# A three-tap convolution by four products for two outputs, in a transformer block on one core

## The chip, the core and the metric

One Trainium2 chip, one core. TensorE (PE, with its weight loads PEld), VectorE (DVE), ScalarE (ACT), GpSimd (POOL) and SyncE's DMA queue (SP) each work through their own list in order and wait for one another by semaphores. The time is that of one launch in device microseconds (us), median of three runs. All data are float32.

## The reference

Eight sequences of 512 tokens, width 256, 16 heads of 16. The block is: layer norm, causal attention, a convolution over the context whose output is a second query, a second attention with the same keys and values, an output projection; then a feed-forward part with a third attention and a mixture of eight experts, two per token. What the change touches is this:

```python
ctx = _causal_attn(q, k, v)
ctx_c = ctx.reshape(b, s, d).transpose(0, 2, 1)
conv_out = jax.lax.conv_general_dilated(ctx_c, conv_w, window_strides=(1,), padding=[(1, 1)],
                                        dimension_numbers=('NCH', 'OIH', 'NCH')) + conv_b[None, :, None]
q2 = conv_out.transpose(0, 2, 1).reshape(b, s, NUM_HEADS, HEAD_DIM)
ctx2 = _causal_attn(q2, k, v)
```

With x the context as a row of columns, padded by a zero column on each side, and g0, g1, g2 the three 256 x 256 taps, output n is g0 x[n] + g1 x[n+1] + g2 x[n+2].

## The kernel before, in words

Sequences are worked in four pairs, 0 to 3; in a pair, `one` has lane 0 and `two` lane 1. `next0` is the first sequence of the next pair, `before1` the second of the pair before. A pair takes 27 turns, and all attention and everything around it lies in these 108 turns. The experts' products follow behind the last turn.

A turn holds two attention steps. Each sequence has three attentions of nine steps, and the two of a pair alternate: `one`'s first attention is turns 0 to 4 and a half, `two`'s first until turn 9, `one`'s second until turn 13 and a half, `two`'s second until turn 18, then the third ones. A step is scores on PE (`sc`, L1201), in two halves, each into one of two score banks; Exp on ACT (L1208), two of 128x1024; a mask on the diagonal blocks on POOL (L1216). The product with the values (`av`, L1134) of earlier steps comes one turn later, between the turn's two score groups. So PE's order in a turn is: scores, AV, `first_units`, scores, `units`. The order on PE, ACT, DVE and POOL is exactly the order in which the program writes the instructions; nothing is moved by a scheduler.

All other work is cut into units, which `plan(turn, sequence, what, ...)` puts into a turn. `among=first_units` puts a unit ahead of the turn's second scores, otherwise it comes behind them. `follow` puts off a piece of work by some turns to one of three places: "mid" (behind AV), "late" (ahead of the units), "end" (behind them).

- When an attention's chunk (of two, 128 rows of the context each) has all its AV, `normalise` copies the two sums out by ACT (L1151), and three DMAs on SP swap halves of their rows (L1159, L1160). `finish` on DVE then does two reciprocals (L1164) and two products (L1165) on 128x256 each: for chunk 0 in the next turn at "mid", for chunk 1 in the same turn at "end". `check` on ACT (L1168) reads the reciprocals; for chunk 1 it stands at "mid" of the next turn, ahead of that turn's second pair of Exps.
- `conv` is six products per output chunk (two input chunks, three taps, L1366) of a 128x128 weight and 512 columns, all into one bank, and one eviction on DVE with the bias (L1374). The six are spread over turns, so the bank is held (`hold_bank`), and the other units have a single bank while it is. Chunk 0 of q2 is needed at the second attention's first step, chunk 1 at its fifth.
- Units of the next sequence: `stats`, `normed` (DVE, L1311), `transpose` (PE L1281, copied by ACT L1285), `q` (PE L1046, DVE L1343), `k` (PE L1046, two on ACT L1330), `values` (PE L1064, DVE L1082). Units of the sequence before: `transpose3`, `route` (PE L1035, then some twenty small DVE operations and one Exp on ACT, L1535), `slots` (PE L1564 and L1565, sixteen small DVE operations, L1567 to L1579). `slots` leaves eight indirect DMAs (L1588) that POOL issues one after each later mask.
- `h` adds the third attention's projection to the rows; the squares for the norm behind it are ACT's (L1502).

An fp32 product is two records of PE in the profile, with a weight load each; half as many matmuls are written as the counts show.

Of the kernel before, what the change touches and what calls it, by code (L numbers as in the profile page):

```python
# [11 lines left out]
F32 = mybir.dt.float32  # L12
# [611 lines left out]
def fast_path(  # L624
# [221 lines left out]
    with ExitStack() as att:  # L846
# [37 lines left out]
        load_x(1)  # L884
        conv_sb = wp.tile([P, DC, 3, D], F32, tag="conv", name="conv_sb")
        context_rows(conv_sb.rearrange("p c k o -> p c (k o)"), convT.rearrange("d k o -> d (k o)"))
        convb_sb = column(conv_b, D, "convb_sb")
# [95 lines left out]

        free_banks = [0, 1]

        def mm_tile():

            i = free_banks.pop(0)
            free_banks.append(i)
            return ps_mm.tile([P, 512], F32, tag=f"mm{i}", name="mm")  # L990

        def hold_bank():
            i = free_banks.pop(0)
            return i, ps_mm.tile([P, 512], F32, tag=f"mm{i}", name="mm")

# [20 lines left out]
        def table(n):  # L1016
            ps = mm_tile()
            for i in range(NC // 2):
                nc.tensor.transpose(ps[:, i * P : (i + 1) * P], rope[0][:, n * NC // 2 + i], ident)
            half = slice(n % 2 * S // 2, (n % 2 + 1) * S // 2)  # L1020
            nc.scalar.copy((cosT, sinT)[n // 2][:, half], ps[:, : S // 2])


# [83 lines left out]
        def follow(turns, f, where):  # L1107
            due[where].append([turns, f])
# [8 lines left out]

        def attention(qT, kT, v, to):

# [24 lines left out]
            def normalise(ch):  # L1144
# [25 lines left out]
                for n0 in range(0, S, S // 2):  # L1170
                    follow(1 - ch, lambda n0=n0: finish(n0), ("mid", "end")[ch])
                follow(3 - 2 * ch, check, ("late", "mid")[ch])

# [70 lines left out]
        class Batch:  # L1244
# [33 lines left out]
            def transposed(self, d, to, of, scale=None, soon=False):  # L1278
                ps = mm_tile()
                for c in range(NC):  # L1280
                    nc.tensor.transpose(  # L1281
                        ps[:, c * P : (c + 1) * P], of[:, c, d * P : (d + 1) * P], ident
                    )
                if scale is None:
                    nc.scalar.copy(to[:, d, :S], ps)  # L1285
                elif soon:
                    nc.vector.tensor_scalar(  # L1287
                        to[:, d, :S], ps, scale[:, d : d + 1], None, ALU.mult
                    )
                else:  # L1290
                    nc.scalar.mul(to[:, d, :S], ps, scale[:, d : d + 1])
# [28 lines left out]

            def transpose(self, d):
                self.transposed(d, self.xT, self.xn)

# [24 lines left out]
            def attention1(self):  # L1348
# [3 lines left out]
                nc.gpsimd.memset(cx[:, :, S + 1 : S + 2], 0.0)  # L1352
                return attention(self.qT, self.kT, self.v, cx[:, :, 1 : S + 1])

            def conv(self, ch, first, n):

                if ch == 0 and first == 0:
                    self.q2T = self.q_tile("q2T")
                    self.held = {}
                if first == 0:  # L1360
                    self.held[ch] = hold_bank()
                bank, ps = self.held[ch]
                terms = [(d, k) for d in range(DC) for k in range(3)]
                for t in range(first, first + n):
                    d, k = terms[t]
                    nc.tensor.matmul(  # L1366
                        ps,
                        conv_sb[:, d, k, ch * P : (ch + 1) * P],
                        self.cx[:, d, k : k + S],
                        start=(t == 0),  # L1370
                        stop=(t == len(terms) - 1),
                    )
                if first + n == len(terms):
                    nc.vector.tensor_scalar(  # L1374
                        self.q2T[:, ch, :], ps, convb_sb[:, ch : ch + 1], None, ALU.add
                    )
                    free_banks.append(bank)

# [113 lines left out]
            def h(self, half):  # L1492
# [7 lines left out]
                for c in range(2 * half, 2 * half + 2):  # L1500
                    squares = small.tile([P, D], F32, tag="squares", name="squares", bufs=1)
                    nc.scalar.activation(  # L1502
                        squares, self.rows[:, c, :D], AF.Square, accum_out=self.ss[:, c : c + 1]
                    )
# [121 lines left out]
        for p in range(B // 2 + 1):  # L1626
# [14 lines left out]
            plan(t + 4, before1, "transpose3", 0, 1)  # L1641
            plan(t + 5, one, "conv", (0, 0, 2), among=first_units)
            plan(t + 5, one, "conv", (0, 2, 1))
            if next0 is not None:
                plan(t + 6, next0, "transpose", 0)
                plan(t + 6, one, "conv", (0, 3, 3))
                plan(t + 6, next0, "transpose", 1)
                plan(t + 6, before1, "route")
                plan(t + 7, one, "conv", (1, 0, 4))
                plan(t + 8, one, "conv", (1, 4, 2))  # L1650
                plan(t + 8, next0, "k", 0)
                plan(t + 9, next0, "q", 0)
                plan(t + 9, next0, "k", 1)
            else:
                plan(t + 6, one, "conv", (1, 0, 3))
                plan(t + 7, one, "conv", (0, 3, 3))
                plan(t + 7, before1, "route")
                plan(t + 8, one, "conv", (1, 3, 3))
            plan(t + 8, before1, "slots")
            plan(t + 10, next0, "values", 0, 1)  # L1660
            for c in range(NC):
                plan(t + 10 + c, one, "bias", c)
                plan(t + 14 + c, two, "bias", c)
            if next0 is not None:
                plan(t + 11, two, "conv", (0, 0, 4))
                plan(t + 12, two, "conv", (0, 4, 2), among=first_units)
                plan(t + 12, two, "conv", (1, 0, 2))
                plan(t + 13, two, "conv", (1, 2, 2))
                plan(t + 14, two, "conv", (1, 4, 1), among=first_units)
                plan(t + 14, two, "conv", (1, 5, 1))  # L1670
            else:
                plan(t + 9, two, "conv", (0, 0, 2))
                plan(t + 10, two, "conv", (0, 2, 1), (1, 0, 1))
                plan(t + 11, two, "conv", (1, 1, 2))
                plan(t + 12, two, "conv", (0, 3, 2), among=first_units)
                plan(t + 12, two, "conv", (0, 5, 1))
                plan(t + 13, two, "conv", (1, 3, 1))
                plan(t + 14, two, "conv", (1, 4, 1), among=first_units)
                plan(t + 14, two, "conv", (1, 5, 1))
            plan(t + 15, one, "x1", 0, 1)  # L1680
# [40 lines left out]
        plan(0, one, "k", 1)  # L1721
        plan(0, one, "q", 1)
        for v in va[1:]:
            units[1].append(lambda v=v: nc.vector.memset(v, 1.0))
# [228 lines left out]
```

## Time and profile before

| what | us |
|---|---|
| three runs | 1468.43, 1470.07, 1470.27 (median 1470.07) |
| the profiled execution | 1469.26, of which the span of instructions is 1467.5 |
| from the first scores to the first product of the experts | 19.7 to 888.6 |
| turns 5 to 14 of pair 0 | 60.29 to 137.90 |
| of pair 1 | 276.73 to 357.57 |
| of pair 2 | 496.71 to 576.61 |
| of pair 3 | 715.47 to 788.68 |

The granted clock is 0.989 over the run. In the stretch of pair 1 (277 to 358), PE is busy for 80.6 of 81 us, ACT 52.3, POOL 36.6 and DVE 34.7. How to read it: a share of busy time says which engine has the most work in all. What a change is worth is read from the starts of the instructions in the turns that it touches. [...]

### The profile page before, as it was taken

The page shows a single profiled execution, that of the slowest core. Times are in us where ns is not written, and L with a number is a line of the kernel's source. Part 1 is how long each engine was busy: PE and PEld are TensorE (multiplying, and loading weights), DVE is VectorE, ACT ScalarE, POOL GpSimd, SP SyncE. Part 2 cuts the span into 40 slices and gives each one's busy share as a digit, 9 for nine tenths or more (in the row PEclk, how much of TensorE's full clock was granted, in tenths as well). Part 3 has the DMA queues.
Part 4 walks back from the last instruction along what each step waited for, and adds up shares of the span by engine and source line. Part 5 has one row for each costly group of instructions (what it writes and reads, how often), then busy time and mean ns, then how long its engine had stood idle before and what let it go on. Part 6 is the DMA issues. An engine that isn't in the chain of part 4 may idle for free. (4 is left out here: it accounts for less than half of the span.)

```text
span 1467.5 us, 31773 instructions
## 1 busy us (share of the span) xinstructions
PE 1420.6 (97%) x13370; PEld 895.6 (61%) x13370; DVE 675.5 (46%) x1318; ACT 726.5 (50%) x1172; POOL 576.9 (39%) x620
## 2 busy tenths in 40 slices
PE   7999999999999999999999999999999999999995
PEld 4555556555556555556555556667767677676673
DVE  4533886553886553886444865322222212222221
ACT  4666677766777766778766784211211211112110
POOL 2333343635333635333645335443332332333322
PEclk9999999999999999999999999999999999999998
DMA  5112122201001211011212022333131313132200
GB/s 145 57 68 79 67 79 85 82 34 42 23 24 52 96 38 38 23 63 38 86 42 76 13 84 68 112 100 96 54 112 44 111 58 98 61 102 88 87 20 17
DMA packets 62840, 97.61 MB, mean 67 GB/s; under 512 B 13516, under 2 KB 39064, under 8 KB 62688
## 3 DMA queue, kind: packets, MB, share of 16 engines
q1 hardware_dynamic: 52608, 69.74, 14.4%
q0 software_dynamic: 10080, 25.74, 5.3%
q8 instruction: 107, 1.75, 0.5%
q14 instruction: 45, 0.37, 0.1%
HBM read 46.06 MB, written 32.61 MB: 54 GB/s over the span
## 5 line engine op out<-in xcount | busy, mean ns | idle before, releaser
L1208 ACT ACTIVATE pr<-sc 128x1024 f32<-128x1024 f32 x432 | 419.1, 1025 | 155.9 <-PE sc L1201 155.6
L1216 POOL TENSOR_TENSOR pr<-pr,seen 128x512 f32<-128x512 f32 (+1 forms) x216 | 253.9, 1176 | 468.2 <-ACT pr L1208 467.8
L762 PE MATMUL pgu<-xgT,gu 128*128 128x384 f32 x1056 | 348.2, 489 | 0.4 <-DVE hT L777 0.3
L762 PEld LDWEIGHTS pgu<-xgT,gu 128*128 128x128 f32 x1056 | 201.2, 191 | 136.3 <-issue 1.5
L776 ACT ACTIVATE sg<-pgu 128x384 f32<-128x384 f32 x120 | 58.9, 491 | 415.6 <-PE pgu L762 415.6
L1134 PE MATMUL av<-pr,va 64*32 64x512 f32 (+7 forms) x6144 | 217.3, 408 | 0.2 <-POOL pr L1216 0.2
L1201 PE MATMUL sc<-qT,kT 32*128 32x448 f32 (+7 forms) x2048 | 194.7, 439 | 6.5 <-ACT pr L1208 5.4
L1164 DVE RECIPROCAL r<-r 128x256 f32<-128x256 f32 x96 | 167.5, 1745 | 57.7 <-DMA r<-cs 57.6
L786 PE MATMUL po<-dn,hT 128*128 128x256 f32 x864 | 190.9, 379 | 1.9 <-POOL hT L757 1.9
L803 POOL DMA_INDIRECT out_dram<-so_far,xg x72 | 72.5, 1006 | 288.5 <-DVE so_far L793 226.1
L777 DVE TENSOR_TENSOR hT<-sg,pgu 128x384 f32<-128x384 f32 x120 | 66.4, 553 | 250.9 <-ACT sg L776 250.9
L786 PEld LDWEIGHTS po<-dn,hT 128*128 128x128 f32 x864 | 162.4, 190 | 23.9 <-POOL hT L757 2.3
L1134 PEld LDWEIGHTS av<-pr,va 64*32 64x32 f32 x6144 | 113.5, 106 | 101.4 <-issue 71.8
L1201 PEld LDWEIGHTS sc<-qT,kT 32*128 32x128 f32 x2048 | 118.3, 185 | 84.9 <-issue 32.8
L793 DVE SCALAR_TENSOR_TENSOR so_far<-po,xg,so_far 128x256 f32<-128x256 f32 x72 | 34.8, 483 | 150.4 <-PE po L786 150.4
L1201 PE MATMUL sc<-q2T,kT 32*128 32x448 f32 (+7 forms) x1024 | 97.3, 434 | 0.7
L748 POOL DMA_INDIRECT so_far<-out_dram,xg x72 | 74.0, 1028 | 53.5 <-issue 51.7
L1366 PE MATMUL mm<-cx,conv_sb 128*128 128x512 f32 x192 | 94.4, 615 | 0.0
L1201 PEld LDWEIGHTS sc<-q2T,kT 32*128 32x128 f32 x1024 | 60.4, 184 | 45.8 <-ACT pr L1208 19.0
L1588 POOL DMA_INDIRECT xtab<-rows,slot x64 | 65.2, 1019 | 36.5 <-DVE pick L1577 19.5
L1046 PE MATMUL mm<-xT,wqkv_sb 128*128 128x512 f32 x128 | 63.7, 629 | 0.0
L1046 PE MATMUL mm<-xaT,wqkv_sb 128*128 128x512 f32 x128 | 61.3, 612 | 2.0 <-DVE xaT L1287 2.0
(159 smaller groups left out, 1284.6 us busy)
## 6 DMA issues: line engine op xcount, KB each, us to landing
r<-cs SPq DMA_DIRECT2D x96, 128.0 KB, 2.0
xtab<-pad SPq DMA_DIRECT2D x24, 397.5 KB, 3.5
xg<-xtab SPq DMA_DIRECT2D x24, 397.5 KB, 3.1
gu<-in_wg_dram SPq DMA_DIRECT2D x18, 352.0 KB, 3.2
cs<-cs SPq DMA_DIRECT2D x48, 128.0 KB, 2.0
gu<-in_wu_dram SPq DMA_DIRECT2D x18, 320.0 KB, 4.1
dn<-in_wd_dram SPq DMA_DIRECT2D x9, 640.0 KB, 4.7
out_dram<-x SPq DMA_DIRECT2D x9, 512.0 KB, 3.0
```

What stands on the lines that cost most here:

```text
L748: nc.gpsimd.indirect_dma_start(out=so_far[:, s, :], out_offset=None, in_=out, in_offset=token_of(xg, s), bounds_check=B * S - 1, oob_is_er ...
L762: nc.tensor.matmul(ps, gu[d][:, n0 : n0 + P], xgT[:, d, :], start=(d == 0), stop=(d == DC - 1),)
L777: nc.vector.tensor_mul(hT[k], sg, pu)
L786: nc.tensor.matmul(po, hT[k][:, s * P : (s + 1) * P], dn[:, k, :], start=(k == 0), stop=(k == NK - 1),)
L803: nc.gpsimd.indirect_dma_start(out=out, out_offset=token_of(xg, s), in_=so_far[:, s, :], in_offset=None, bounds_check=B * S - 1, oob_is_er ...
L1046: nc.tensor.matmul(ps, w[:, d, n0 : n0 + P], srcT[:, d, :S], start=(d == 0), stop=(d == DC - 1),)
L1134: nc.tensor.matmul(av[i][g * HP : (g + 1) * HP, j * KB :], v[rows, j, ch * G + g, :], pr[rows, g, at : at + n], start=(j == 0), stop=(j == ...
L1164: nc.vector.reciprocal(r[:, half], r[:, half])
L1201: nc.tensor.matmul(sc[:, g - g0, at : at + S - j * KB], kT[r0 : r0 + HP, ch, j], qT[r0 : r0 + HP, ch, j * KB : S], start=True, stop=True,)
L1208: nc.scalar.activation(pr[:, g0 : g0 + 2], sc, AF.Exp, scale=SCALE)
L1216: nc.gpsimd.tensor_tensor(diag, diag, seen.unsqueeze(1).unsqueeze(1).to_broadcast([P, G, len(parts), KB]), ALU.mult,).ins
L1366: nc.tensor.matmul(ps, conv_sb[:, d, k, ch * P : (ch + 1) * P], self.cx[:, d, k : k + S], start=(t == 0), stop=(t == len(terms) - 1),)
```

## The change

Two outputs, an even and an odd one, are made of four products of half the columns. With a, b, c, d four neighbouring columns of the context, the terms are a - c, b + c, d - b, c - b, and the weights g0, (g0 + g1 + g2)/2, g2, (g0 - g1 + g2)/2. The output of the even column is M0 + M1 + M3, that of the odd column M1 - M3 + M2. DVE makes the terms (`differences`, four operations on 128x256 with inputs at a step of two) when a chunk of the first attention is finished. The weights are made once, in turn 2 of pair 0. In `conv`, ACT copies M1 out with the bias, DVE makes M1 + M3 and M1 - M3, then adds M0 and M2 into the columns of q2.

A conv's products (four per bank) are no longer spread, no bank is held, and the two banks of units alternate always. The transposes of the next sequence are copied by DVE instead of ACT in turn 5. The terms of `one` take the buffer of the next sequence's keys, those of `two` the buffers of `rows` and `xn` of lane 0. The squares of `h` go into the bank of the projection instead of a buffer of their own.

```diff
-        conv_sb = wp.tile([P, DC, 3, D], F32, tag="conv", name="conv_sb")
+        conv_sb = wp.tile([P, DC, 4, D], F32, tag="conv", name="conv_sb")
...
-        free_banks = [0, 1]
+        banks = itertools.count()
 
         def mm_tile():
-            i = free_banks.pop(0)
-            free_banks.append(i)
-            return ps_mm.tile([P, 512], F32, tag=f"mm{i}", name="mm")
-
-        def hold_bank():
-            i = free_banks.pop(0)
-            return i, ps_mm.tile([P, 512], F32, tag=f"mm{i}", name="mm")
+            return ps_mm.tile([P, 512], F32, tag=f"mm{next(banks) % 2}", name="mm")
...
+        def conv_weights():
+            g = [conv_sb[:, :, k] for k in range(4)]
+            nc.vector.tensor_tensor(g[3], g[0], g[2], ALU.add)
+            nc.vector.tensor_tensor(g[3], g[3], g[1], ALU.subtract)
+            nc.vector.scalar_tensor_tensor(g[1], g[1], 2.0, g[3], ALU.mult, ALU.add)
+            for k in (1, 3):
+                nc.vector.tensor_scalar(g[k], g[k], 0.5, None, ALU.mult)
...
                 for n0 in range(0, S, S // 2):
                     follow(1 - ch, lambda n0=n0: finish(n0), ("mid", "end")[ch])
+                if then is not None:
+                    follow(1 - ch, lambda: then(ch), ("mid", "end")[ch])
                 follow(3 - 2 * ch, check, ("late", "mid")[ch])
...
-                    nc.scalar.copy(to[:, d, :S], ps)
+                    (nc.vector.tensor_copy if soon else nc.scalar.copy)(to[:, d, :S], ps)
...
+            def differences(self, d):
+                if self.lane == 0:
+                    tag = f"kT{2 - self.set}"
...
+                else:
+                    tag = ("rows0", "xn0")[d]
+                    t = big.tile([P, 4, S // 2], F32, tag=tag, name="terms", bufs=1)
...
+                nc.vector.tensor_tensor(t[:, 0], even[:, :n], even[:, 1:], ALU.subtract)
+                nc.vector.tensor_tensor(t[:, 1], odd[:, :n], even[:, 1:], ALU.add)
+                nc.vector.tensor_tensor(t[:, 2], odd[:, 1:], odd[:, :n], ALU.subtract)
+                nc.vector.tensor_tensor(t[:, 3], even[:, 1:], odd[:, :n], ALU.subtract)
 
-            def conv(self, ch, first, n):
+            def conv(self, ch, pair):
...
+                ps = mm_tile().rearrange("p (k n) -> p k n", k=2)
+                for i, k in enumerate(((1, 3), (0, 2))[pair]):
+                    for d in range(DC):
+                        nc.tensor.matmul(
+                            ps[:, i],
+                            conv_sb[:, d, k, ch * P : (ch + 1) * P],
+                            self.terms[d][:, k],
+                            start=(d == 0),
+                            stop=(d == DC - 1),
+                        )
+                if pair == 0:
+                    m1 = small.tile([P, S], F32, tag="t0", name="t0", bufs=3)[:, : S // 2]
+                    nc.scalar.activation(
+                        m1, ps[:, 0], AF.Identity, bias=convb_sb[:, ch : ch + 1]
                     )
+                    t = self.m = small.tile([P, 2, S // 2], F32, tag="t1", name="t1", bufs=2)
+                    for i, op in enumerate((ALU.add, ALU.subtract)):
+                        nc.vector.tensor_tensor(t[:, i], m1, ps[:, 1], op)
+                else:
+                    to = self.q2T[:, ch].rearrange("p (n i) -> p i n", i=2)
+                    for i in range(2):
+                        nc.vector.tensor_tensor(to[:, i], self.m[:, i], ps[:, i], ALU.add)
...
-            plan(t + 5, one, "conv", (0, 0, 2), among=first_units)
-            plan(t + 5, one, "conv", (0, 2, 1))
             if next0 is not None:
-                plan(t + 6, next0, "transpose", 0)
-                plan(t + 6, one, "conv", (0, 3, 3))
-                plan(t + 6, next0, "transpose", 1)
+                plan(t + 5, next0, "transpose", (0, True), (1, True), among=first_units)
+                plan(t + 5, next0, "q", 0)
                 plan(t + 6, before1, "route")
-                plan(t + 7, one, "conv", (1, 0, 4))
-                plan(t + 8, one, "conv", (1, 4, 2))
-                plan(t + 8, next0, "k", 0)
-                plan(t + 9, next0, "q", 0)
-                plan(t + 9, next0, "k", 1)
             else:
-                plan(t + 6, one, "conv", (1, 0, 3))
-                plan(t + 7, one, "conv", (0, 3, 3))
-                plan(t + 7, before1, "route")
-                plan(t + 8, one, "conv", (1, 3, 3))
-            plan(t + 8, before1, "slots")
-            plan(t + 10, next0, "values", 0, 1)
+                plan(t + 5, before1, "route", among=first_units)
+            plan(t + 7, one, "conv", (0, 0), (0, 1))
+            plan(t + 8, one, "conv", (1, 0), (1, 1))
+            plan(t + 9, next0, "k", 0)
+            plan(t + 9, before1, "slots")
+            plan(t + 10, next0, "values", 0)
+            plan(t + 11, next0, "values", 1)
...
-            if next0 is not None:
-                plan(t + 11, two, "conv", (0, 0, 4))
...
+            plan(t + 12, two, "conv", (0, 0), among=first_units)
+            plan(t + 12, two, "conv", (0, 1))
+            plan(t + 13, next0, "k", 1)
+            plan(t + 14, two, "conv", (1, 0), among=first_units)
+            plan(t + 14, two, "conv", (1, 1))
```

## The prediction

> **What bounds the kernel now.** I read the page's shares first, then the timeline of PE, then those of ACT and DVE where PE waits.
>
> ```profile
> PE 1420.6 (97%) x13370; PEld 895.6 (61%) x13370; DVE 675.5 (46%) x1318; ACT 726.5 (50%) x1172; POOL 576.9 (39%) x620
> ...
> L1366 PE MATMUL mm<-cx,conv_sb 128*128 128x512 f32 x192 | 94.4, 615 | 0.0
> ```
>
> PE is the bound, and the convolution is 94.4 us of it. But ends of matmuls are modelled, so waits hide in a busy PE. I therefore go by starts in the timeline (columns: start, length, engine, line, tiles, count):
>
> ```profile
> 363.56 3.72 PE L1035 MATMUL mm<-outw_sb,c 128*128 128x256 f32 x16
> 367.21 1.14 PE L1201 MATMUL sc<-q2T,kT 32*128 32x512 f32 x8
> ...
> 770.34 1.98 PE L1366 MATMUL mm<-cx,conv_sb 128*128 128x512 f32 x4
> 772.26 1.17 PE L1201 MATMUL sc<-q2T,kT 32*128 32x384 f32 x16
> 773.36 1.12 PE L1366 MATMUL mm<-cx,conv_sb 128*128 128x512 f32 x2
> 774.59 2.05 PE L1201 MATMUL sc<-q2T,kT 32*128 32x320 f32 x16
> 776.58 3.41 PE L1134 MATMUL av<-pr,va 64*32 64x512 f32 x96
> ```
>
> Sixteen products of 256 columns take 3.65 us from start to next start (363.56 to 367.21), four of 512 take 1.92, two 1.24. Scores (L1201) of one step take 1.10, but 1.99 (774.59 to 776.58) when only 1.24 us of other work stood before them: they need the score bank that the step before filled, and ACT's Exp of it must end. From the first score of a step to the last of the next pass about 4.33 us (1.10 + 1.24 + 1.99), or 1.10 + 1.91 + 1.34. So "filler plus next scores" is never under 3.23 us: PE work taken out below 2.1 us of filler saves nothing.
>
> ```profile
> 756.63 1.94 ACT L1208 ACTIVATE pr<-sc 128x1024 f32<-128x1024 f32 x2 [1.32 <-PE sc L1201]
> 759.79 0.63 ACT L1168 ACTIVATE cs<-r 128x512 f32<-128x512 f32 x1 [1.23 <-issue]
> ...
> 760.42 1.92 ACT L1208 ACTIVATE pr<-sc 128x1024 f32<-128x1024 f32 x2
> ```
>
> ```profile
> 752.45 0.15 DVE L1567 TENSOR_TENSOR at<-run,mm 128x8 f32<-128x8 f32 x1
> ...
> 755.49 0.17 DVE L1579 CAST slot<-red 128x4 int32<-128x4 f32 x1
> 755.57 1.75 DVE L1164 RECIPROCAL r<-r 128x256 f32<-128x256 f32 x1
> 757.56 0.48 DVE L1165 TENSOR_TENSOR cx<-cs,r 128x256 f32<-128x256 f32 x1 [0.24 <-DMA cs<-cs]
> 757.97 1.74 DVE L1164 RECIPROCAL r<-r 128x256 f32<-128x256 f32 x1
> ```
>
> This is turn 10 of the last pair (scores at 755.37). ACT's check L1168 needs both reciprocals and stands in ACT's order ahead of the turn's second pair of Exps: slots on DVE 3.1 us, then 4.2 us from the first reciprocal to the check, then 0.63 to the Exps.
>
> **The change, part by part.** Times of turns 5 to 14 before, from first score to first score of turn 15: pairs 0 to 3 take 77.6 (60.29 to 137.90), 80.8 (276.73 to 357.57), 79.9 (496.71 to 576.61) and 73.2 (715.47 to 788.68).
>
> *Products.* A pair has 48 conv records of 512 columns and gets 64 of 256. In a run, starts are 0.43 apart for 512 columns (weight loads at 74.95, 75.38, 75.81) and 0.216 for 256 ((3.65 - 0.2)/16, 0.2 being what a run adds: 1.92 - 4 x 0.43). That is 20.6 against 13.8 us per pair, 27 us over four pairs: the whole possible gain. New blocks: eight records 1.92, sixteen 3.65.
>
> *The new order, turn by turn, for the middle pairs 1 and 2* (scores, AV, scores, units; rows of the same turn before, 1.34 for scores behind a filler of 1.9):
> - 5: 2.04 + 1.02 + 1.24 (eight transposes) + wait 1.6 + 1.10 + q 1.91 = 8.9 (before 7.3).
> - 6: 1.34 + 2.90 + 1.10 + route 1.88 = 7.2 (before 11.9, with transposes queueing for one bank).
> - 7: 1.34 + 1.46 + 1.83 + 3.65, + 0.3 = 8.6 (8.9 and 8.0).
> - 8: 1.10 + 2.31 + 1.10 + 3.65 = 8.2 (8.5).
> - 9: 1.07 + 1.94 + 1.34 + k and slots 2.3 = 6.6 (8.0).
> - 10 and 11: 1.10 + 1.88 + 1.53 + 1.9, then 1.34 + 1.94 + 1.27 + 1.9 = 12.9, + wait 2.9 = 15.8 (16.1).
> - 12, 13, 14: 6.9, 7.7, 7.3 (6.7, 7.6, 5.8), and turn 15 opens with 1.34 instead of 1.98.
> Sum 77.2 - 0.6 = 76.6: a gain of 4.2 and 3.3.
>
> *The wait in turn 5.* The four differences of a chunk stand on DVE between the reciprocals and normed:
>
> ```profile
> 278.37 0.43 DVE L1165 TENSOR_TENSOR cx<-cs,r 128x256 f32<-128x256 f32 x1
> 278.71 1.38 DVE L1311 TENSOR_SCALAR xn<-x,mv,rstd 128x256 f32<-128x256 f32 x4
> ```
>
> One costs 0.43 as L1165 alone does, at 0.45 spacing 1.8 us. Normed ends at 281.9 instead of 280.1; the transposes, now in turn 5 right behind AV (279.79), need it. Scores can start at 282.65 instead of 281.03: 1.6 us. Queued behind on DVE are the two new xT copies (0.65 each) and q; PE needs the copies only after 1.10 of scores. In pair 0 normed would end at 60.2 (58.4 before) for an AV that ends at 63.4; pair 3 has no next chunk.
>
> *The 0.3 in turn 7.* Reciprocals now queue behind q's eviction and end 5 us into turn 6, so the second chunk's differences end about 1 us into turn 7, route's chain starts there, and ACT's small Exp of route (L1535, waits for DVE) holds the score Exps behind it.
>
> *The wait in turn 10.* Slots move to turn 9's end, directly ahead of the reciprocals. With t the first score of turn 10: slots end t + 3.15, check at t + 7.35, Exps t + 8.0 to 9.9, scores of turn 11 end t + 10.65 where 7.75 was due: 2.9. Pair 3 has less filler (due 9.33), so 1.3. Pair 0 has no slots, and its scores lose nothing. Slots' eight indirect transfers on POOL (L1588, 1.02 each, one behind each mask) move with it from turns 9 to 12 into 10 to 13: with two masks (1.27) and a bias (0.74) POOL then has 5.3 us per turn, and the shortest such turn is 5.75 in pair 3. If that cover were gone, AV would wait for its mask.
>
> *Pair 0:* 7.3, 5.35 (no unit in turn 6), 10.15 (scores 3.23 for it), 8.2, 6.3, 6.65, 6.45, 6.9, 7.7, 7.3 = 72.2, less 0.6: gain 6.0. *Pair 3:* turns 6, 10, 11 and 13 have no unit, so 3.23 each time: 6.0, 7.2, 9.7, 8.2, 4.95, 6.1, 6.5, 8.7, 5.75, 9.2 = 72.3, + 1.3 - 0.6: gain 0.2.
>
> *Costed at nothing, with the cover:* making the weights (five operations of 512 elements, about 2.9 us) lies in DVE's gap 38.8 to 43.3; without it values' eviction in turn 2 is that late. The m1 copy on ACT (0.37 as L1021) and the four half adds per chunk (0.43 to 0.48 by L1165 and L793, against one 0.75) end 2 us or more before their bank or q2T is asked for. Squares into PSUM keep 0.42 each (L1502) and hold the bank until then; turn 3's q comes about 1 us after. The terms share buffers: with the next chunk's k, which on PE comes behind the last product that reads them; with rows, whose transfers are through two turns before; with xn, read in turn 5 and rewritten in 9. No wait from these as long as the turns keep this order; else DVE's differences would be late by a transfer, 2 to 3 us. Bounds for all this together: -1 to +3.
>
> Sum: 4.2 + 3.3 + 6.0 + 0.2 = 13.7; I take back 0.6 for DVE operations that meet a mask on POOL in turn 5 (0.75 instead of 0.43 below). From 1469.3 for the profiled run (span 1467.5 and 1.8 around it) that is 1456; the median of 1470.07 lies 0.8 higher, so 1457.
>
> ```profile
> 69.42 0.75 DVE L1165 TENSOR_TENSOR cx<-cs,r 128x256 f32<-128x256 f32 x1 [0.26 <-DMA cs<-cs]
> ```
>
> *Bounds of a difference.* L1165 spans 0.424 to 1.473 us. No row reads two operands at step 2; L954 reduces 128 elements at step 2 in 0.275, L950 the same number in rows of eight in 0.279, so I take no stride cost, nearest 0.43. At 1.47 turn 5 is 4.2 later and turn 7 about 3.5 in two pairs, and pair 0 some 1.
>
> [...]
>
> **The rivals.**
> - *The waits hide, all arithmetic comes through* (20%). If normed and slots were not the last to arrive, 3.2 + 5.8 + 1.3 + 0.6 + 0.6 come back: 1446. For it: before, the check in turn 10 of pair 1 came without idle. Against: in pair 3 it held the Exps, as shown.
> - *Each pair loses 3 us more at the Exp floor* (10%): 1469, no change. For: ACT's order is strict, and turns get shorter while its work stays. Against: ACT is busy 52 of 81 us there.
> - *POOL holds every difference* (8%), slower: each waits for a mask or an indirect transfer. Price 2 x (4.2 + 3.5) + 1 = 16.4 over the forecast: 1473.5; it decides from about 1.4 us per difference. For: L1165's maximum. Against: its median, 0.427.
> - *Half-long products do not hide their weight load* (4%), slower: loads take 0.19 and 256 columns 0.216. At 0.32 instead of 0.216 per record, 256 records cost 27 us more: 1484. For: only 26 ns of slack. Against: L1035 and L786 run at 0.216.
>
> **How the numbers follow.** The forecast, 1457, has 56%; 2% is for the rest. 1446 to 1468 leaves out the slower cases and part of the third. A difference under 0.2% (2.9 us) can't be told from none. Faster: 56 + 20 + 2; same: 10; slower: 12.
>
> **What would show it.** Right: L1396 records 0.216 apart; PE's transposes in turn 5 of pairs 1 and 2 waiting for DVE xn by 1.6; ACT's check in turn 10 idle on DVE and the Exps behind it 8 us into the turn; scores near 2 to 3 us where no unit stands before. Wrong: differences over 0.6, no idle before the check, turns 16 to 26 or the expert stage changed by over 1 us, or a wait at the first half adds of the convolution.

## The result, and the profile after

Twelve runs of each kernel: 1469.63 us after (1464.60 to 1475.35), 1470.20 before; the ratio is 0.9992, 95% interval 0.9975 to 1.0008. That is no change. The forecast was 1457. The profiled execution took 1468.78, with a span of 1466.9.

The page of the kernel after, shares and the convolution's groups:

```profile
PE 1404.1 (96%) x13434; PEld 914.2 (62%) x13434; DVE 718.6 (49%) x1441; ACT 728.8 (50%) x1182; POOL 579.3 (39%) x620
...
L1396 PE MATMUL mm<-terms,conv_sb 128*128 128x256 f32 x256 | 61.7, 389 | 0.0
```

The convolution's busy time fell from 94.4 to 61.7 us, and PE's share from 97% to 96%, in the same span. So the products did get cheaper, and something took the time back. The view of windows, one line for turns 5 to 14 of each pair (start and end, length, busy time of PE, PEld, DVE, ACT and POOL, granted clock, then the DMA's share and GB/s), shows where. Before:

```profile
60.29:137.90 77.61, 77.38 (x965) 41.42 (x965) 23.86 (x25) 51.11 (x77) 25.46 (x24) 1.00 0.22 77
276.73:357.57 80.84, 80.43 (x984) 43.89 (x985) 34.54 (x69) 52.15 (x78) 36.63 (x35) 0.98 0.12 44
496.71:576.61 79.90, 79.49 (x985) 44.08 (x985) 34.75 (x70) 52.06 (x78) 36.70 (x35) 1.00 0.12 44
715.47:788.68 73.21, 71.67 (x901) 38.06 (x901) 29.08 (x60) 48.30 (x72) 36.56 (x35) 1.00 0.15 53
```

After:

```profile
58.30:131.00 72.70, 71.53 (x980) 45.65 (x980) 31.52 (x49) 52.30 (x79) 25.51 (x24) 0.98 0.24 83
268.87:348.90 80.03, 75.75 (x1000) 48.90 (x1000) 45.10 (x97) 53.01 (x80) 36.73 (x35) 0.96 0.12 44
487.69:570.43 82.74, 77.05 (x1000) 49.42 (x1000) 44.87 (x99) 52.99 (x80) 37.06 (x35) 0.94 0.12 44
709.25:789.23 79.98, 71.38 (x916) 44.17 (x917) 35.88 (x81) 50.75 (x76) 36.78 (x35) 0.89 0.16 54
```

Pair 0 gained 4.9 us here (6.1 over all its turns). Pairs 1 and 2 have 4 to 6 us in which PE does nothing, pair 3 has 8.6, and the granted clock falls from pair to pair: 0.98, 0.96, 0.94, 0.89. In these two profiles the recorded clock is either full or half, and in the turns half comes in stretches of 3.41 us, one or two of them in a row. Counted over all 108 turns there are 3 such windows before and 13 after (1, 2, 4 and 6 in pairs 0 to 3).

Lengths from first score to first score, worked out from the starts (a star marks a turn with a half-clock window in it, or just ahead):

| turns | before | forecast | after |
|---|---|---|---|
| 5 of pairs 1, 2 | 7.3, 7.3 | 8.9 | 11.17*, 12.21* |
| 6 of pairs 1, 2 | 11.9, 11.9 | 7.2 | 6.98, 7.21 |
| 10 + 11 of pairs 1, 2 | 16.1, 16.1 | 15.8 | 17.22*, 17.23* |
| 5 to 14 of pair 0 | 77.6 | 72.2 | 72.7* |
| 5, 6 of pair 3 | 7.3, 8.8 | 6.0, 7.2 | 7.28, 9.77* |
| 10, 11 of pair 3 | 6.5, 6.5 | 7.4, 6.5 | 10.23*, 8.43* |
| all 108 | 868.9 | 855.8 | 873.0 |

The turns are 4.1 us longer than before. The first scores come 2.0 us sooner (17.7 against 19.7), and what follows the turns is 2.7 us shorter (half clock for 3.4 us near 890, where before has 6.8 near 921). So the span is the same. These 4.7 us need not be the change's: over the profiles of the kernels below that are built on it, the first scores come at 17.8 to 19.6 us, and what follows the turns takes 574.5 to 578.9, with nothing altered in either place.

The waits are where the forecast put them. Turn 5 of pair 1 after, timeline of PE and then of DVE (start, length; idle before and its releaser in brackets):

```profile
270.91 1.09 PE L1138 MATMUL av<-pr,va 64*32 64x320 f32 x32
272.85 0.56 PE L1287 MATMUL mm<-ident,xn 128*128 128x128 f32 x2 [0.85 <-ACT pr L1214]
274.37 1.09 PE L1287 MATMUL mm<-ident,xn 128*128 128x128 f32 x6 [0.95 <-DVE xn L1317]
275.39 1.77 PE L1207 MATMUL sc<-qT,kT 32*128 32x384 f32 x16
277.09 3.03 PE L1050 MATMUL mm<-xT,wqkv_sb 128*128 128x512 f32 x4
```

```profile
270.93 0.43 DVE L1384 TENSOR_TENSOR terms<-cx 128x256 f32<-128x256 f32 x1
...
271.94 0.44 DVE L1387 TENSOR_TENSOR terms<-cx 128x256 f32<-128x256 f32 x1
272.28 2.36 DVE L1317 TENSOR_SCALAR xn<-x,mv,rstd 128x256 f32<-128x256 f32 x4
```

The four differences come 0.34 apart, normed stands behind them, and the transposes wait for it. PE stands idle for 0.85 and 0.95 us there (forecast 1.6); the profile names normed for the second and ACT's Exp for the first. Normed took 2.36 here instead of 1.38, beside a mask on POOL (1.35 us, from 272.81). And then q: four records of 512 columns in 3.03 us, which take 1.98 at full clock (at 274.48 in the run with normed a turn earlier, below). The window from 275.8 to 279.2 has half clock.

Turn 10 of the same pair (from 309.81), the timeline of ACT, then one line of DVE's and one of PE's:

```profile
311.07 1.94 ACT L1214 ACTIVATE pr<-sc 128x1024 f32<-128x1024 f32 x2
316.88 0.63 ACT L1172 ACTIVATE cs<-r 128x512 f32<-128x512 f32 x1 [3.88 <-issue]
...
317.51 1.92 ACT L1214 ACTIVATE pr<-sc 128x1024 f32<-128x1024 f32 x2
```

```profile
315.06 1.75 DVE L1168 RECIPROCAL r<-r 128x256 f32<-128x256 f32 x1
```

```profile
318.57 2.36 PE L1207 MATMUL sc<-q2T,kT 32*128 32x256 f32 x16 [2.47 <-ACT pr L1214]
```

ACT stands idle for 3.88 us ahead of the check, which starts 7.07 us into the turn, as the second reciprocal ends (316.81); the forecast had 7.35. The profile names no releaser for it (`issue`), so that it waits for DVE is read from these times. PE waits 2.47 us for the Exps behind it, and the next window, 320.2 to 323.6, is at half clock:

```profile
316.80:320.20 3.40, 1.63 (x14) 1.39 (x16) 3.15 (x8) 3.31 (x7) 0.61 (x1) 1.00 0.00 0
320.20:323.60 3.40, 3.40 (x52) 1.33 (x58) 0.00 (x0) 1.78 (x2) 3.21 (x4) 0.50 0.14 45
323.60:327.00 3.40, 3.40 (x64) 2.17 (x48) 0.00 (x0) 1.71 (x2) 1.42 (x2) 1.00 0.11 40
```

In these lines PE was busy 1.63 of 3.40 us at full clock, then all of 3.40 at half clock.

### The profile page after: what moved, and what is told of

Same layout as the page of the kernel before. It is cut to its first block, busy times and chain, and to the rows that moved or that the text cites. A ratio compares the mean times of both kernels' runs of the same rounds, so it can differ in the third digit from the quotient of the medians.

```text
span 1466.9 us, 32054 instructions
## 1 busy us (share of the span) xinstructions
PE 1404.1 (96%) x13434; PEld 914.2 (62%) x13434; DVE 718.6 (49%) x1441; ACT 728.8 (50%) x1182; POOL 579.3 (39%) x620
## 5 line engine op out<-in xcount | busy, mean ns | idle before, releaser
L1138 PE MATMUL av<-pr,va 64*32 64x64 f32 (+7 forms) x6144 | 227.9, 423 | 0.0
L1207 PE MATMUL sc<-qT,kT 32*128 32x192 f32 (+7 forms) x2048 | 196.9, 442 | 9.2 <-ACT pr L1214 8.7
L1138 PEld LDWEIGHTS av<-pr,va 64*32 64x32 f32 x6144 | 116.6, 109 | 108.2 <-issue 77.8
L1207 PE MATMUL sc<-q2T,kT 32*128 32x128 f32 (+7 forms) x1024 | 99.0, 439 | 11.2 <-ACT pr L1214 11.2
L1396 PE MATMUL mm<-terms,conv_sb 128*128 128x256 f32 x256 | 61.7, 389 | 0.0
```

What stands on the lines that cost most here:

```text
L1138: nc.tensor.matmul(av[i][g * HP : (g + 1) * HP, j * KB :], v[rows, j, ch * G + g, :], pr[rows, g, at : at + n], start=(j == 0), stop=(j == ...
L1207: nc.tensor.matmul(sc[:, g - g0, at : at + S - j * KB], kT[r0 : r0 + HP, ch, j], qT[r0 : r0 + HP, ch, j * KB : S], start=True, stop=True,)
```

## The experiments

Three theories. W: waits made by VectorE's order, and behind them a clock that halves. P: the same waits, each worth only its own length. C: cheaper products are worth nothing in this kernel. Each kernel below is the changed kernel with the edit shown, unless its paragraph says otherwise. Ratios are to the kernel before, which had medians of 1470.8, 1467.7 and 1466.8 in the three groups of runs; they are the record's, and lie up to 0.0015 off the quotients of the medians. The interval is of 95%. Turn lengths and windows are each from one profiled execution.

**Normed ahead of the differences.** Chunk 0's differences are put behind the units.

```diff
-                    follow(1 - ch, lambda: then(ch), ("mid", "end")[ch])
+                    follow(1 - ch, lambda: then(ch), "end")
```

> The changed kernel, with the differences of a sequence's first chunk put behind the units of turn 4 instead of ahead of them, so that on VectorE normed comes before them. Theory W (VectorE's order makes TensorE wait, in turn 5 for normed and in turns 10 and 11 for the Exps behind the check, and each wait lowers the granted clock in the next 3.4 us, which doubles its price): turn 5 of pairs 1 and 2, 11.2 and 12.2 us after the change, falls to 7.3 to 7.6, the half-clock window there goes (275.8 to 279.2 in pair 1), and the time falls by 7 to 9 us to about 1462. Rival P (the waits cost only themselves, the clock is by the way): turn 5 falls by the wait alone, 1.6 to 2.5 each, time 1465 to 1467. Rival C (the cheaper products are worth nothing because other engines bound these turns): what turn 5 gains is lost in turns 6 and 7, time 1469 to 1471.

1465.00 (ratio 0.9956, 0.9940 to 0.9971). In pair 1 turn 5 is 7.24 instead of 11.17, and its window is gone. In pair 2 it is still 11.93: the row swap's DMA lands later there (its first reciprocal waits 3.34 us for it, and the second DMA another 1.08), so normed, still behind the products, ends late anyway. The order of the two was the cause in pair 1, not the whole of it in pair 2. Of the 3.9 us of turn 5, pair 1 as a whole keeps 1.0: half-clock windows now stand in its turn 7 (9.27 instead of 8.00) and its turn 11 (two, 9.45 instead of 8.46). The time is P's number (1465 to 1467), not W's (about 1462).

**The check behind the Exps.** Only chunk 1's check of the first attention moves.

```diff
-                follow(3 - 2 * ch, check, ("late", "mid")[ch])
+                follow(3 - 2 * ch, check, "late" if then is not None else ("late", "mid")[ch])
```

> The changed kernel, with the check of the first attention's second chunk moved on ScalarE from ahead of the second pair of Exps of the turn to behind it. Theory W: turns 10 and 11 of pairs 1 and 2 fall from 17.2 to about 12.9 us each, of pair 3 from 18.7 to 12.5 to 14; the half-clock windows at 320, 542, 757 and 760 go; time down by 11 to 14 us to about 1456 to 1459. Rival P: they fall by 2.9, 2.9 and 1.3 us, time 1462 to 1464. Rival C: no change of the time.

1455.71 (0.990, 0.987 to 0.993). Turns 10 and 11 of pairs 1 and 2 are 6.22 and 6.46, 4.5 us less per pair than with the wait and its window. The forecast's price of this wait was 2.9. W's number (1456 to 1459) nearly held, P's (1462 to 1464) did not. Turn 10 of pair 3 falls from 10.23 to 6.20. One moved read of 0.63 us on ACT, which nothing waits for but the Exps in its queue, is worth some 14 us.

**Slots back in turn 8.**

```diff
+            plan(t + 8, before1, "slots")
             plan(t + 8, one, "conv", (1, 0), (1, 1))
             plan(t + 9, next0, "k", 0)
-            plan(t + 9, before1, "slots")
```

> The changed kernel, with slots of the sequence before put back to turn 8 (ahead of the convolution's products there), so that its sixteen operations on VectorE no longer stand ahead of the reciprocals of turn 9. Theory W: the check in turn 10 comes about 3 us earlier in pairs 1 to 3, turns 10 and 11 fall to 13 to 13.5 in pairs 1 and 2 and to about 14 in pair 3; time 1458 to 1462. Rival P: 1463 to 1465. If instead the check waits for the transfers of the swapped rows and not for slots, nothing changes.

1466.60 (0.9977, 0.9954 to 1.0001): next to nothing. The wait leaves turn 10 of pair 1 (6.40), but the convolution's second bank waits 1.28 us for DVE in turn 8 (10.1 us instead of 8.2), and in pair 2 turns 10 and 11 stay at 8.51 and 9.97. Removing what stood ahead of the reciprocals is not the same as freeing the Exps from the check. Both theories had expected more (W 1458 to 1462, P 1463 to 1465).

**More work in the waits.** Products of 256 columns that nobody reads are added: 44 of them, two records each, 19 us of PE by 88 x 0.216, in turns 5 and 10 of pairs 1 and 2 and in turns 5, 6, 9, 10 (twice as many), 11 and 13 of pair 3.

```diff
+        def spare(n):
+            ps = mm_tile()
+            for _ in range(n):
+                nc.tensor.matmul(
+                    ps[:, :256], conv_sb[:, 0, 0, :P], conv_sb[:, 1, 0, :256], start=True, stop=True
+                )
...
+                    first_units[t + 5].append(lambda: spare(4))
...
+                units[t + 10].append(lambda: spare(4))
```

> The changed kernel, with products that nobody reads added where TensorE waits or has no unit: four of 256 columns (1.9 us) ahead of the transposes in turn 5 of pairs 1 and 2, behind values in turn 10 of pairs 1 and 2, and in turns 5, 6, 9, 10, 11 and 13 of pair 3: 19 us of products in all. Theory W: they lie in waits, the granted clock stays up, and the time falls although there is more work: turn 5 of pairs 1 and 2 by 1 to 2 us, pair 3 by 4 to 8; time 1456 to 1465. Rival P (clock by the way): the products fill waits at best, time 1469 to 1475. Rival C: TensorE is not the limit of these turns, the time stays at 1469 to 1471.

1462.04 (0.9932, 0.9909 to 0.9955): 19 us of work more, and faster than the changed kernel, whose interval does not touch this one. Windows of half clock in the turns go from 13 to 4. Its turns 5 to 14, same view as above:

```profile
58.94:131.66 72.72, 71.55 (x981) 45.66 (x981) 31.49 (x49) 52.27 (x79) 25.45 (x24) 0.98 0.24 83
270.69:348.17 77.48, 76.68 (x1016) 50.76 (x1016) 45.24 (x97) 52.92 (x80) 36.66 (x35) 1.00 0.13 45
486.05:567.22 81.17, 78.45 (x1017) 51.55 (x1017) 44.49 (x98) 52.87 (x80) 37.15 (x35) 0.98 0.12 43
706.23:783.21 76.98, 75.59 (x973) 51.07 (x973) 35.14 (x81) 50.28 (x76) 36.74 (x35) 1.00 0.17 60
```

The clock of pair 3 goes from 0.89 to 1.00 and its length from 79.98 to 76.98. What a window costs can be read off one turn: turn 10 of pair 1 is 8.76 with the spare products and without, but turn 11 behind it is 7.36 instead of 8.46 (and 6.89 in pair 2 of the run at full price below, with no window and no spare products). Its AV, 64 records, takes 2.48 us here and 3.27 in the half-clock window. P can't explain this run (it had 1469 to 1475): the waits are all still there, only filled.

**Normed a turn earlier.**

```diff
-            plan(t + 4, next0, "normed")
+            plan(t + 3, next0, "normed")
...
-        plan(4, later, "normed")
+        plan(3, later, "normed")
```

> The changed kernel, with normed of the next sequence moved from the units of turn 4 to those of turn 3, so that on VectorE it stands ahead of the reciprocals, which wait for the row swaps by DMA (in pair 2 these land 1.1 us later than in pair 1, behind a 512 KB load and a store). Theory W: the transposes of turn 5 wait for nothing in pairs 1 and 2 alike, turn 5 is 7.1 to 7.6 us in both (11.2 and 12.2 after the change), its half-clock windows go, time 1460 to 1463. Rival P: turn 5 falls by the wait alone, time 1464 to 1466. If the length of pair 2's turn 5 is not due to normed behind the late reciprocals, it stays at 11 to 12.

1462.64 (0.9975, 0.9958 to 0.9992). The time is in W's range, but turn 5 is a miss: 9.12 and 11.21, not 7.1 to 7.6. The transposes no longer wait, but q does. Pair 1, timeline of DVE, then of PE:

```profile
271.45 1.38 DVE L1384 TENSOR_TENSOR terms<-cx 128x256 f32<-128x256 f32 x1
...
273.75 1.27 DVE L1291 COPY xT<-mm 128x512 f32<-128x512 f32 x2
```

```profile
274.48 1.98 PE L1050 MATMUL mm<-xT,wqkv_sb 128*128 128x512 f32 x4 [1.95 <-DVE xT L1291]
```

The transposes' copies, moved to DVE by the change, queue behind the same differences. The forecast named them as queued there, and gave PE 1.10 us of scores as the cover; that is too little.

**Both: normed earlier and the check behind the Exps.**

> The changed kernel with normed in turn 3 and the check of the second chunk behind the Exps: both waits away. Theory W: pairs 1 and 2 take 211 to 213 us each (217.9 and 222.1 after the change), the time is 1447 to 1451. Rival P: 1455 to 1460.

1452.23 (0.9897, 0.9865 to 0.9930). Pairs 1 and 2 take 213.6 and 214.8; before they took 220.0 and 218.8. Pairs and time are a little over W's ranges (211 to 213, 1447 to 1451); P had 1455 to 1460.

**Pair 3 with its convolution spread.** As the last one; where there is no next pair, the four banks of `one` go to turns 7, 8, 8 and 9, those of `two` to 11, 12, 13 and 14, slots to 10. The first kernel has no more than that; the second has 20 unread products too, in turns 5, 6, 10, 12 and 14 of pair 3.

```diff
+            else:
+                plan(t + 7, one, "conv", (0, 0))
+                plan(t + 8, one, "conv", (0, 1), among=first_units)
+                plan(t + 8, one, "conv", (1, 0))
+                plan(t + 9, one, "conv", (1, 1))
+                plan(t + 10, before1, "slots")
```

> The same without the spare products. Theory W: where no unit stands between the scores of two steps TensorE idles, the granted clock falls by half for windows of 3.4 us between 700 and 800, pair 3 takes 213 to 217 us, and the time is 2 to 6 us above that with the spare products. Rival P: the same time as with them.

> As the one before, and in the last pair the convolution is spread over turns 7 to 14, one bank at a time, slots in turn 10, with 1.9 us of products that nobody reads in turns 5, 6, 10, 12 and 14, which have no unit left. Theory W: pair 3 takes 209 to 212 us (218.4 after the change), no half-clock window between 700 and 800; time 1440 to 1445. Rival P: the spare products bring nothing over the same kernel without them.

1447.40 (0.9861, 0.9830 to 0.9893) without, 1444.85 (0.9851, 0.9822 to 0.9880) with them. Pair 3 takes 210.7 and 207.4 (before 209.5, after 218.4), both less than W expected (213 to 217, 209 to 212); between 700 and 800 us the first has 3 windows of half clock, the second none. The 8.6 us of unread products cost nothing; that they gain is seen in pair 3's turns, not for certain in the time.

**The differences behind the copies.** As the kernel with the spread and the unread products, and the differences of chunk 0 later, ahead of the units of turn 5 instead of behind AV in turn 4; in the first kernel the copies are on ACT again. (The expectation says 80 unread products; it is 20, in 40 records.)

```diff
-                    follow(1 - ch, lambda: then(ch), ("mid", "end")[ch])
+                    follow(2 - 2 * ch, lambda: then(ch), ("late", "end")[ch])
...
-                plan(t + 5, next0, "transpose", (0, True), (1, True), among=first_units)
+                plan(t + 5, next0, "transpose", 0, 1, among=first_units)
```

> This is the version with normed in turn 3, the check behind the Exps, pair 3's convolution spread over turns 7 to 14 and 80 products that nobody reads in pair 3, with two more edits: the first chunk's differences come one place later (ahead of the units of turn 5, not behind AV), and the two copies of the transposed rows in turn 5 are ACT's again. It asks whether the wait that is left in turn 5 of pairs 1 and 2 (10.8 and 9.6 us long; q waits 1.95 us for the copies, which queue behind the differences on VectorE) is VectorE's order. Theory W (waits by VectorE's order, plus the clock that halves behind them): turn 5 at 7.5 to 8.5 in pairs 1 and 2, the half-clock windows near 276 and 491 gone, turn 7 or 8 not over 0.5 longer; turns 5 and 6 together 3 to 5 us shorter over the two pairs; 1440 to 1443 us. Rival P (a wait costs only its own length): 2 us, about 1443. If the copies on ACT hold the Exps instead, turn 5 stays over 9 and ACT shows the idle time.

> As the version with the copies on ACT, but with the copies on VectorE, as the change has them, now ahead of the first chunk's differences in its order. It tells the place of the differences from the engine of the copies. Theory W: the copies still stand behind two reciprocals and two products, so they end about 1.5 to 2.5 us sooner than in the version without these edits, turn 5 of pairs 1 and 2 is 8 to 9.5, and the windows near 276 and 491 go in at least one of the two pairs; 1441 to 1444 us. Rival P: 1443 to 1444. Differences that end too late would show as a longer turn 7.

1441.04 (0.9836, 0.9816 to 0.9857) with ACT's copies, 1438.33 (0.9820, 0.9796 to 0.9844) with DVE's. Turn 5 is 7.44 in both pairs, and 7.10. So the copies' engine did not matter; the place of the differences did, and more than expected for DVE (8 to 9.5). The second is the fastest version, 1.8% under the kernel before. Its turns 5 to 14:

```profile
58.69:131.20 72.51, 71.04 (x981) 45.13 (x981) 33.05 (x54) 52.19 (x79) 25.53 (x24) 0.98 0.23 83
268.81:340.38 71.57, 71.57 (x1000) 47.21 (x1001) 47.55 (x95) 52.73 (x80) 37.09 (x35) 1.00 0.14 50
479.14:551.62 72.48, 72.48 (x1000) 47.18 (x1000) 43.34 (x95) 52.97 (x80) 37.49 (x35) 0.98 0.14 51
689.25:760.16 70.91, 70.91 (x956) 47.73 (x957) 40.85 (x88) 50.63 (x76) 36.90 (x34) 1.00 0.16 57
```

The profile shows no idle time of PE left in pairs 1 to 3, and 8.5, 10.3 and 9.1 us are gone against the kernel after. DVE has as much to do as there.

**Cheaper products in the old order.** The kernel before, with the middle tap's products left out (four products per chunk instead of six; q2 lacks the tap).

```diff
                     d, k = terms[t]
+                    if k == 1:
+                        continue
```

> The kernel before, in its own order, with the middle tap's products left out (four products of 512 columns per output chunk instead of six; the middle tap is missing from q2). TensorE so has the same 27 us less to do as in the change, and nothing else moves. It asks what cheaper products are worth alone. Theory W: where they are taken out, the scores behind them meet the Exp floor of 3.23 us for filler and scores, and a part comes back as waits: by that floor, turns 5, 7, 8 and 11 to 14 give 3 to 5 us per pair, 12 to 20 in all, and some half-clock windows appear (5 to 10 instead of 3), which take 3 to 12 us back: 1452 to 1464. Rival P (waits cost only themselves): 1450 to 1458 with no more windows than before. Rival C (cheaper products are worth nothing in this kernel): 1468 to 1471.

1454.41 (0.9930, 0.9906 to 0.9954). C falls. PE has 27 us less to do, and 12.8 come out in the turns: per pair 4.5, 6.0, 3.6 and, in pair 3, -1.3. Less than half; in pair 3 turns 10 and 11 even get longer (6.47 to 8.67, 6.54 to 7.80). I read that as the floor of Exp and scores, which this run does not show by itself; pair 3 also has 3 windows where it had none, one of them in turn 11. Between W and P it does not decide: there are 5 windows instead of 3.

**Full price in the new order.** The changed kernel with the first product of each group written twice, 96 records of 256 columns per pair instead of 64.

```diff
-                    for d in range(DC):
+                    for again, d in ((True, 0), (False, 0), (False, 1)):
...
-                            stop=(d == DC - 1),
+                            stop=(again or d == DC - 1),
```

> The changed kernel with its first product of each group written twice (the second one is what counts), so that the convolution has 96 records of 256 columns per pair instead of 64: 20.6 us per pair, as much TensorE time as before the change, in the new order. It asks what the saved products are worth inside the change. Rival P: 27 us more where none of it stands in a wait, about 1490 to 1497. Theory W: TensorE has waits and half-clock windows in these turns (13 windows, 45 us), and more work ahead of the scores takes some of both away: 1478 to 1492, with fewer windows than the change has. Theory C: 1468 to 1472. Whatever it costs above the kernel before is what the new order with its waits costs at equal work: W expects 8 to 22 us.

1497.09 (1.0220, 1.0195 to 1.0245). Against the changed kernel the span is 25.5 us longer, where the products cost 27.6 more (128 x 0.216). So P's number (1490 to 1497) held, at its edge, and W's 1478 to 1492 missed: the work added lies on the path nearly whole, and the windows hardly change (11). The turns of the four pairs, less those of the kernel before, are -1.2, +8.0, +6.7 and +15.9 us: at equal PE work the new order costs nothing in pair 0 and 31 us in the others, where W had 8 to 22 in all. So the products' 27 us did come, and the order took them back.

## Why the prediction was wrong

*The products* were sized right: 1.92 and 3.65 us per block, 27 us in all, and the run at full price shows that this comes through in the new order. *The differences* too: their median was 0.42 to 0.43 us, the row of L1165. Single ones beside a mask on POOL took 1.4 to 1.5 (in pair 2, at 491.8: 1.49), so the rival "POOL holds every difference" is out as written, though pairs 1 and 2 each pay one such meeting in turn 5 (pair 1's falls on normed), for which 0.6 had been taken back in all.

*Pair 0* gained 6.1 us, as forecast (6.0). It is the pair without the two waits. Some of the agreement is chance: its turn 7 is 9.85 with a window in it (forecast 10.15), and 8.23 in a run without one there.

*The two waits* were found, with their cause and place: transposes idle on normed in turn 5, the Exps held by the check in turn 10. *The step that failed is their price, and that of pair 3's turns without a unit: the sum counted each wait at its own length, at the clock of the kernel before.* The runs show in its place:

- Half clock came behind some of PE's waits (from 275.8 and 320.2, above). The same turns were seen with and without a window: turn 7 of pair 0 (9.85 and 8.23), turn 7 of pair 2 (9.20 and 8.00), turn 11 in the run at full price (8.46 in pair 1, 6.89 in pair 2), turn 25 of pair 2 (7.76 and 7.21). So a window costs 0.6 to 1.6 us, by what lies in it. Repeated runs of one kernel give much the same: over the 117 executions of 14 kernels with a span and a clock on record, each group of runs taken about its own mean, 0.001 less of the mean granted clock goes with 1.06 us more of span, which is 1.2 us per window. The twelve runs of the kernel after have a mean clock of 0.980, 19 runs of the kernel before 0.989: some 9 of the 12.6 us missed. Both are estimates, and a fit is no experiment; the spare products are one, and they took 9 of the 13 windows and 6.6 us out of the turns, 19 us of added work notwithstanding.
- The wait in turns 10 and 11 was 2.9 in the forecast, and by itself that is right: in pair 2 of the run at full price it stands unfilled and without a window, and the two turns take 15.6, against 12.7 with the check behind the Exps. With its window they take 17.2, 1.4 over the forecast in each of two pairs.
- The wait in turn 5 is 2.3 and 3.3 us over. In pair 1, 1.7 of it goes in the run with spare products, which has no window there (9.51), and normed beside the mask took 1.0 longer than the forecast had. In pair 2 the row swap also lands late. Before, the first reciprocal in this place waits 2.21 us for it, after 3.26. There the transposes stood a turn later, and it did not matter: the change took that slack out, and the forecast worked its turn 5 from pair 1 alone.
- Pair 3 was to gain 0.2 and lost 8.9, half of the miss. Its turns 5, 6, 10, 11 and 13 have little or nothing behind the scores, and it has 6 of the 13 windows. The check's wait there was 1.3 by the forecast; turn 10 went from 6.20 to 10.23 with it, of which 1.9 goes when the waits are filled and no window is left (8.32 with spare products). Turn 5 was mis-sized without any window: 7.28 in every run without added products there, not 6.0, since the scores that open turn 6 wait for the Exp floor too.

By pairs the turns miss the forecast by 0, 2, 7 and 9 us, 4.7 come back outside them, and that is the 12.6 between 1457 and 1469.6. One of the forecast's own signs of error (over 1 us outside turns 5 to 14) came: turns 16 and 24 of pair 3 are 1.1 and 1.7 longer, the expert stage 2.7 shorter.

The rival "each pair loses 3 us more at the Exp floor" gave the right number, 1469, but not the mechanism: pair 0 lost nothing and pair 3 nine. What stays open: the split between wait and clock over the whole run is an estimate, since no run held the clock at full rate with all the waits unfilled. Turn 0 of pair 2 is 1.1 us longer in most runs of the new order, and turn 16 of pair 3 by as much in the kernel after; neither has a window, and their causes were not tried.

## What to carry to other kernels

Work taken off the bounding engine is worth its price only if what fed that engine can come sooner by as much; list what stands in front of the feeding operation on its own queue, and move consumers with slack (a check, terms that are needed two turns later) behind it before counting the gain. Price a wait on TensorE with the clock that may halve behind it: here a wait of 2.5 us of PE, with its window, was worth 4.5 (turns 10 and 11). And look at the granted clock stage by stage: over the run 0.989 and 0.979 look alike, and yet 0.001 went with about 1 us.

## What was not expected of the hardware

- In the profile of the kernel after, half clock starts on a grid of 3.41 us (275.8, 320.2, 494.3 and 507.9 are 13, 51 and 4 steps apart). One drop, at 320.2, followed a window with PE busy for 1.63 of 3.40 us. Not every wait was followed by one: the same wait in pair 2 of the run at full price (2.46 us, up to 559.37) did not, though PE was busy for only 1.41 of 3.40 us there.
- A drop also followed PE work without any wait. In pair 2 after, the window from 507.9 to 511.3 has half clock, behind AV, scores and sixteen products of 8 columns:

```profile
504.13 1.17 PE L1207 MATMUL sc<-qT,kT 32*128 32x256 f32 x16
505.23 1.95 PE L1039 MATMUL mm<-wr_sb,xmT 128*128 128x8 f32 x16
507.11 1.85 PE L1207 MATMUL sc<-qT,kT 32*128 32x512 f32 x8
```

  The scores in the last line take 1.85 us there, 1.14 at full clock (before, at 367.21). PE is busy for all 3.40 us of the window ahead of 507.9, and for 1.63 of the one ahead of 320.2, so its busy time does not tell where a drop follows.
- The traces agree on a sum that does. Give each record its columns times 0.84 ns (0.43 us for 512, the distance of starts before) and the size of the tile in its line as a share of `128*128`: all for that, a quarter for scores (`32*128`), an eighth for AV (`64*32`). Between 20 and 860 us, the 14 traces have 3334 grid windows at full clock. The 84 that half clock followed sum to at most 0.38 of their length; all but 4 of the other 3250 have more, the median 0.83. Half-clock windows part at the same place: the 17 that another follows have at most 0.37, the 82 behind which full clock returns at least 0.41. The window ahead of 320.2 has 0.20, the one ahead of 507.9 has 0.37, and the one at full price without a drop 0.39. So in these traces the drops go with this sum. It was fitted after the runs (records taken 0.1 us behind their start), and no run varied it alone: that a low sum is the cause is not shown.
- 19 us more of PE work made a kernel 8 us faster (1462.04 with the unread products, 1469.63 without).
